# Causal attention on one core: another order of the query blocks, and one block's last norm moved into the recurrence

## The chip, the cores and the metric

The kernel runs on one core of one Trainium2 chip. The metric is the device time of one execution in microseconds (us), taken on the slowest core, of which there is one here. The core has five engines that run their own instruction streams and wait for each other by semaphores: TensorE (PE; its weight loads are listed apart as PEld), VectorE (DVE), ScalarE (ACT), GpSimd (POOL) and SyncE (SP), which here issues most of the DMAs.

## The reference, cut to what matters

The input x has 2 sequences (batches) of 2048 rows of 256 numbers. Six layers add to it in turn:

```
x = x + 0.5 * moe(layernorm(x))
x = x + attention0(layernorm(x))         # full attention, 16 heads
x = x + 0.5 * moe(layernorm(x))
x = x + 0.5 * recurrence(layernorm(x))
x = x + attention1(layernorm(x))         # the changed one
x = x + 0.5 * recurrence(layernorm(x))
```

The changed layer is causal attention with 16 heads of 16 numbers, rotated queries and keys, and a learned vector per clipped distance (-32 to 32) in both the scores and the sum:

```
q, k = rotate(x @ w_q.T) / 4, rotate(x @ w_k.T);  v = x @ w_v.T
rel = rel_emb[clip(key - query, -32, 32) + 32]
scores = q . k + q . rel, masked where key > query
a = softmax(scores)
out = (a @ v + sum over keys of a * rel) @ w_o.T
```

The layer after it, the recurrence, goes over the two sequences as its two steps, row by row of the 2048:

```
c = sigmoid(x@wf.T + c@uf.T + bf) * c + sigmoid(x@wi.T + c@ui.T + bi) * tanh(x@wc.T + c@uc.T + bc)
h = tanh(x @ wo.T + c_last @ uo.T + bo)
```

## The kernel before

**Layout.** x stays on the chip for the whole program as 8 blocks of 512 rows (4 chunks of 128 rows): blocks 0 to 3 are batch 0, blocks 4 to 7 batch 1 (SB = 4 blocks a batch). A layer norm of a block has three calls (L95 to L127): `stats` (mean and variance on DVE, the root on POOL in `root`, `ve` and `rstd`), `normal` (four operations, x to normalised rows `b`) and `turn` (eight transposes on PE and two ACT copies). n4 is the norm ahead of the causal attention, n5 the one ahead of the last recurrence.

**Groups.** `attention1` (from L1008) cuts its work into 32 groups (b, qc, g): batch b, query block qc of 512 queries (the "first" block is qc = 0, the "fourth" qc = 3), and one of G = 4 sets of four heads. The list `groups` fixes their order. Before, each batch has the second block's four groups, then the third block and the first block in turns for pairs of groups (2, 2, 0, 0, 2, 2, 0, 0), then the fourth block's four.

**Units.** Each group is done twice over the keys. The first pass, "largest", makes scores on PE (L1149) and their row maxima on DVE (L1158, and L1179 to L1192 near the diagonal, where the distance term is added from a `band` buffer, of which there are NBAND = 3). The negated maxima `mneg` are transposed and added to the queries by `subtract` (L645). The second pass, "exponential", makes the scores again with keys on the partitions (L1243, L1250, L1260, L1266), takes their exponential on ACT (L1274), and one unit later multiplies by the values in `weighted` (L1283). ACT copies that product to a buffer `part` (L654; five buffers) and POOL adds it to the group's sum one unit later (L552). Each pass of a group takes 4*qc + 3 units: 3 for the first block, 15 for the fourth. A unit may hold a piece of "largest" of one group, a piece of "exponential" of an earlier one, or both; PE's instructions of both are issued in alternation by the loop over units (L1401 to L1424).

**The planner.** The lists Ms and Me (first and last unit of a group's "largest"), Es and Ee (of its "exponential") and By come from fixed rules (L1317 to L1332): "exponential" starts at least three units after the group's "largest" has ended and after the previous group's; "largest" starts when a band buffer is free, and every second group from the sixth on not before the "exponential" of five groups earlier has ended plus nine units:

```
start = max(start, free + 9 - size)
if n > 5 and n % 2 == 0:
    start = max(start, Ee[n - 5] + 9)
...
start = Me[-1] + 3
if n:
    start = max(start, Ee[-1] + 1)
```

**Small jobs.** All else is put into units by distance from those numbers (L1350 to L1398): projections `queries`, `keys` (rotated on POOL, two at a time) and `vals`; the norms of blocks (`ln_stats`, `ln_transpose`); `tables` (cosine and sine of a block, by DMA); `by_position` (distance scores of a group, stored to DRAM and loaded back in skewed form by `band_load`); and after the maxima `band_store`, `positions_load`, `positions_exp`, `positions_T` (four transposes, L1306) and `positions` (one product, L1311), which handle the distance term of the sum. `divide` (L661, transposes at L668) comes at `end = max(Es + 13, Ee + 4)`. When a block's fourth group is divided, `outputs_T` (L682) follows at end + 2 and `outputs`, in two halves (L691), at end + 4 and end + 6; these add the layer's result to x. Jobs that fall behind the last "exponential" unit are simply done one after the other there, a stretch called the drain below. DMA issues that SP makes are `sends` at units of the same plan. At the end the list `tail` (L1551, put into the plan at L1398) adds the norms of blocks 0 and 4 for the last recurrence, at Me of the last group plus 6 to 14 units.

**The last recurrence** (L865 to L1005) has its order written out by hand. Per block cb and step it has a `gate` for each half m (three products, ACT's functions, DVE's state update, L921). Its `normal` and `turn` make a block's norm only where it is not there yet (L891 to L899). The beginning reads:

```
normal(0, 0); first_bias(); turn(0, 0); normal(1, 0)
gate(0, 0, 0); turn(1, 0); gate(0, 0, 1); normal(0, 1)
gate(1, 0, 0); turn(0, 1); gate(1, 0, 1)
```

Here normal(0, 0) is block 0 and normal(0, 1) block 4, the first block of batch 1. `first_bias` (L881) holds the recurrence's first matmuls. Its weights are loaded on SP, issued behind the attention's own DMAs (L1461, L1559).

## Time and profile before

| what | value |
| --- | --- |
| median of 5 runs | 4149.44 us (4145.87 to 4153.36) |
| profiled execution | 4146.6 us, span 4144.8 us |
| mean granted TensorE clock | 0.983 |
| causal attention, from the timeline | 2686.6 to 3961.4 us of the span |
| last recurrence, from the timeline | 3961.4 us to the end |

The profile is one execution. Times in it are us from the start of the span. The page gives each engine's busy time as a share of the span, then the span in 40 slices with the busy tenths of each engine and the granted TensorE clock, then the chain of work that ended last. A group "out<-in" names an instruction by the program's buffers, and Lnnn is the line of the kernel. The view of windows gives the same for any stretch; the timeline gives single instructions or runs of them, with the idle time ahead of them and what ended it.

### The profile page before, as it was taken

What the parts mean: (1) busy time and instruction counts of PE and PEld (TensorE: products, weight loads), DVE (VectorE), ACT (ScalarE), POOL (GpSimd) and SP (SyncE); (2) the same over time, 40 slices, a digit from 0 to 9 for tenths busy, and PEclk for the clock granted to TensorE, in tenths of its full rate; (3) what the DMA queues carried; (4) which work ended last, traced back from release to release, by engine and by line L of the source; (5) the groups of instructions that cost most, each with busy time, mean ns of one, the idle gap of its engine ahead of it and who ended that gap; (6) DMA issues with size and microseconds to landing.
All of it is one profiled execution on the core that took longest, in us unless ns stands there. A gap on an engine that the chain in (4) does not pass through costs nothing.

```text
span 4144.8 us, 78045 instructions
## 1 busy us (share of the span) xinstructions
PE 4003.9 (97%) x29024; PEld 1966.7 (47%) x29024; DVE 2700.2 (65%) x6131; ACT 2555.0 (62%) x5067; POOL 1621.8 (39%) x1421
## 2 busy tenths in 40 slices
PE   7899999999999999999996999999999999999999
PEld 4455433333333433333343554655555455555445
DVE  5234888888877788888742234477767756767634
ACT  2233588888888788888851332256666776676842
POOL 4234233335433333333344123044554564544410
PEclk9899999999999999999998999999999999999999
DMA  7232000100000000000022331054543343542201
GB/s 246 91 117 76 24 2 1 47 1 1 2 1 1 1 1 1 1 1 1 10 92 90 98 108 44 11 113 77 113 95 70 77 83 77 113 95 60 69 1 41
DMA packets 355514, 223.28 MB, mean 54 GB/s; under 512 B 146624, under 2 KB 338496, under 8 KB 355136
## 3 DMA queue, kind: packets, MB, share of 16 engines
q1 hardware_dynamic: 276800, 176.33, 16.7%
q0 software_dynamic: 12288, 33.57, 2.5%
q10 hardware_dynamic: 66048, 8.39, 1.4%
q8 instruction: 231, 3.78, 0.4%
q14 instruction: 147, 1.20, 0.1%
HBM read 113.12 MB, written 105.12 MB: 53 GB/s over the span
## 4 chain that ended last, share of the span: by engine, by line
PE 90%; DVE 4%; another core or an unknown queue 3%; ACT 2%; issue 2%; POOL 0%; DMA 0%; ACTq 0%; DVEq 0%; POOLq 0%
PE s L780 14%; PE s L792 12%; PE s L766 10%; PE s L148 7%; PE s L1149 7%; PE s L1283 7%; PE s L394 6%; PE s L1250 6%; PE s L414 3%; PE s L157 3%; PE s L1260 1%; PE s L691 1%; PE s L1243 1%; PE s L1266 1%
## 5 line engine op out<-in xcount | busy, mean ns | idle before, releaser
L552 POOL TENSOR_TENSOR part<-part 128x512 f32<-128x512 f32 (+2 forms) x768 | 950.1, 1238 | 1395.6 <-ACT part L654 1391.7
L770 DVE TENSOR_REDUCE mx<-s 128x1 f32<-128x512 f32 x2048 | 1271.3, 684 | 301.6 <-PE s L766 290.8
L785 ACT ACTIVATE pT<-s 128x512 f32<-128x512 f32 x2048 | 1063.5, 617 | 197.8 <-PE s L766 194.6
L766 PE MATMUL s<-kT,q 32*128 32x512 f32 x4096 | 1029.4, 617 | 1.7 <-issue 0.8
L780 PE MATMUL s<-q,kT 32*128 32x512 f32 x4096 | 1017.5, 615 | 1.3 <-DVE q L649 1.3
L1274 ACT ACTIVATE pT<-s 128x512 f32<-128x512 f32 (+1 forms) x1152 | 580.6, 584 | 207.7 <-PE s L1250 103.0
L780 PEld LDWEIGHTS s<-q,kT 32*128 32x128 f32 x4096 | 416.0, 183 | 460.9 <-DVE mx L770 376.5
L654 ACT COPY part<-s 128x512 f32<-128x512 f32 (+2 forms) x832 | 500.3, 602 | 164.9 <-PE s L792 58.3
L1158 DVE TENSOR_REDUCE mx<-s 128x1 f32<-128x512 f32 (+1 forms) x768 | 472.7, 679 | 155.4 <-PE s L1149 149.7
L792 PE MATMUL s<-pT,v 128*32 128x512 f32 x4096 | 549.2, 604 | 0.7 <-ACT pT L785 0.2
L766 PEld LDWEIGHTS s<-kT,q 32*128 32x128 f32 x4096 | 410.4, 183 | 140.6 <-ACT pT L785 78.3
L1149 PE MATMUL s<-kT,q 32*128 32x160 f32 (+6 forms) x2240 | 341.3, 429 | 0.0
L394 PE MATMUL s<-we,xT 128*128 x592 | 292.3, 618 | 18.7 <-issue 12.3
L1283 PE MATMUL s<-pT,v 128*32 128x512 f32 (+3 forms) x2560 | 297.3, 539 | 5.0 <-ACT pT L1274 4.8
L401 DVE TENSOR_TENSOR h<-sg,s 128x256 f32<-128x256 f32 x148 | 62.4, 421 | 358.0 <-ACT sg L399 305.9
L1149 PE MATMUL s<-b,q 32*128 32x512 f32 (+7 forms) x1280 | 261.0, 515 | 1.8 <-DVE mx L1158 1.8
L447 POOL DMA_INDIRECT yg<-results,at x128 | 126.1, 985 | 329.0 <-DMA results<-y 243.0
L792 PEld LDWEIGHTS s<-pT,v 128*32 128x32 f32 x4096 | 84.4, 108 | 351.0 <-ACT pT L785 327.6
L1250 PE MATMUL s<-q,kT 32*128 32x512 f32 (+3 forms) x1152 | 242.1, 508 | 0.0
L552 POOL TENSOR_TENSOR band<-band,mneg 128x640 f32<-128x640 f32 x128 | 160.2, 1262 | 154.5 <-DVE mneg L1192 85.0
L1179 DVE CUSTOM_DVE_ANT_0 band<-s,band 128x160 f32<-128x160 f32 (+1 forms) x512 | 153.7, 314 | 96.0 <-PE s L1149 60.8
L1250 PE MATMUL s<-q,b 32*128 32x512 f32 (+3 forms) x896 | 212.0, 568 | 0.0
(227 smaller groups left out, 5181.2 us busy)
## 6 DMA issues: line engine op xcount, KB each, us to landing
band<-skew SPq DMA_DIRECT2D x32, 1280.0 KB
pd<-band SPq DMA_DIRECT2D x32, 1280.0 KB
xs<-places SPq DMA_DIRECT2D x148, 128.0 KB
results<-y SPq DMA_DIRECT2D x148, 128.0 KB
places<-zero SPq DMA_DIRECT2D x2, 4736.0 KB
we<-in_we SPq DMA_DIRECT2D x12, 768.0 KB
skew<-s ACTq DMA_DIRECT2D x32, 256.0 KB
s<-pd SPq DMA_DIRECT2D x32, 256.0 KB
```

The lines of the kernel that those rows point to most:

```text
L394: nc.tensor.matmul(pu, lhsT=xT[n][:, ts(kc, P)], rhs=w[:, kc, ds(val[n], 2 * D)], start=kc == 0, stop=kc == 1,)
L552: fn(*args)
L654: nc.scalar.copy(part[:, q0:], pv[:, q0:])
L766: nc.tensor.matmul(ps, lhsT=q[t][rows(j), ts(qb, P)], rhs=kT[b, g][rows(j), ts(kc, TB)], start=True, stop=True,)
L770: nc.vector.tensor_reduce(mx[t][:, qb * J + j, kc : kc + 1], ps, AX.X, ALU.max)
L780: nc.tensor.matmul(st, lhsT=kT[b, g][rows(j), ts(kb, P)], rhs=q[t][rows(j), :], start=True, stop=True,)
L785: nc.scalar.activation(z.pTs[t, kb, j], st, AF.Exp)
L792: nc.tensor.matmul(pv[rows(j), :], lhsT=v[b, g // 2][:, kb, ds(h * VW, 32)], rhs=z.pTs.pop((t, kb, j)), start=True, stop=True,)
L1149: nc.tensor.matmul(ps[:, ds(cols, n)], lhsT=q[t][rows(j), ts(qb, P)], rhs=kT[b, c, g][rows(j), ds(k0, n)], start=True, stop=True,)
L1250: nc.tensor.matmul(ps[:, q0:], lhsT=k, rhs=q[t][rows(j), q0:], start=True, stop=True, skip_group_check=True,)
L1274: nc.scalar.activation(z.pTs[t, kbs, j][:, q0:], ps[:, q0:], AF.Exp)
L1283: nc.tensor.matmul(pv[rows(j), q0:], lhsT=v[b, kb // CPB, g // 2][:, kb % CPB, ds(h * VW, 32)], rhs=pT[:, ds(c0, TB - q0)], start=kb == kb ...
```

## The change

The first block is no longer alternated with the third block but with the fourth, so that a batch goes second (four groups), third (four groups), then fourth and first in turns for pairs of groups. With this, the last groups of the program are two of the first block of batch 1, and that block's x is complete only at the end of the attention; its norm for the last recurrence leaves the list `tail`, and is made by the recurrence's own `normal(0, 1)` and `turn(0, 1)`. The norm of block 0 stays in `tail`, at Me of the last group plus 2, 4 and 6 units. The tables of the fourth block wait for the projections of the third block where they waited for those of the first.

```
-                groups += [(b, 1, g) for g in range(G)]
+                groups += [(b, qc, g) for qc in (1, 2) for g in range(G)]
                 for g in range(0, G, 2):
-                    groups += [(b, qc, g + i) for qc in (2, 0) for i in range(2)]
-                groups += [(b, 3, g) for g in range(G)]
+                    groups += [(b, qc, g + i) for qc in (3, 0) for i in range(2)]
...
-                    done_ = {2: 1, 3: 0}.get(qc)
+                    done_ = {2: 1, 3: 2}.get(qc)
...
-        tail = []
-        for i, b in enumerate((0, SB)):
-            tail += [(3 + 2 * i, n5.stats, b), (4 + 2 * i, n5.normal, b, nc.vector),
-                     (5 + 2 * i, n5.turn, b)]
+        tail = [(1, n5.stats, 0), (2, n5.normal, 0, nc.vector), (3, n5.turn, 0)]
```

Everything else that moves does so through the planner's rules, which are unchanged.

## The prediction

> **What bounds the kernel now.** I read the page's busy shares first, then its slices, then the chain that ended last: TensorE (PE) is busy 97% of the span and carries 90% of the chain, so a microsecond counts only where PE has less to do or is left waiting.

> ```profile
> PE 4003.9 (97%) x29024; PEld 1966.7 (47%) x29024; DVE 2700.2 (65%) x6131; ACT 2555.0 (62%) x5067; POOL 1621.8 (39%) x1421
> ...
> PE   7899999999999999999996999999999999999999
> ...
> PEclk9899999999999999999998999999999999999999
> ...
> PE 90%; DVE 4%; another core or an unknown queue 3%; ACT 2%; issue 2%; POOL 0%; DMA 0%; ACTq 0%; DVEq 0%; POOLq 0%
> ```

> By the timeline the causal attention runs from 2686.6 to 3961.4, the last recurrence from there to the end. Next, the windows (start:end, length, then busy time and count of PE, PEld, DVE, ACT, POOL; granted clock; DMA share; GB/s), one for 100 us of the attention and three for single units of the plan: "largest" alone, "largest" paired with "exponential", "exponential" alone.

> ```profile
> 3600.00:3700.00 100.00, 99.31 (x956) 57.40 (x949) 70.42 (x238) 69.73 (x138) 51.83 (x44) 1.00 0.56 115
> 2857.68:2859.34 1.66, 1.66 (x14) 0.73 (x13) 1.62 (x8) 0.43 (x3) 0.70 (x2) 1.00 0.00 0
> 3804.30:3807.23 2.93, 2.93 (x26) 1.00 (x25) 2.42 (x5) 1.96 (x5) 1.43 (x2) 1.00 1.16 265
> 3945.69:3948.29 2.60, 2.60 (x20) 0.74 (x16) 0.00 (x0) 2.60 (x7) 0.45 (x2) 1.00 0.00 0
> ```

> PE is full in the paired unit (2.93) with DVE and ACT to spare. Alone, "largest" takes 1.66, all but 0.04 of it DVE's maxima, and "exponential" 2.60, all of it ACT's. So a pair costs 2.93 where the two alone cost 4.26: each further pair saves up to 1.3 us, because a lone unit runs at the pace of DVE or ACT.

> **Part 1, the order of groups.** No matmul of the scores is added or removed; only their places change. I worked the planner's rules (starts, ends, band buffers) through for both orders. Before: 257 units hold both pieces, 31 only "exponential", 31 only "largest". After: 261, 27, 27. So four more pairs. Price: with 2.60 for the lone "exponential" 1.33 each; the fastest one in that stretch starts at 3943.62 and the next at 3945.69, 2.07, which gives 0.80. Four times: −5.3 to −3.2. I take the middle, **−4.2**. Units near the diagonal (band work on DVE) also meet other partners; I fitted the lengths of before's units by kind of piece and by small jobs (residual 0.29 a unit), and these shifts came to +4.5 and −4.1, so I put them at **0 (±2)**.

> **Part 2, the end of the attention.** Before, the last group has 15 units and most of its small jobs fall among them; after, the last two groups are first-block groups of 3 units, and what is due at fixed distances falls behind the last "exponential" unit. Now the view of the stretch behind it and its timeline (start, length, engine, line, operation, wait before):

> ```profile
> 3906.72:3950.75 44.03, 44.03 (x371) 16.73 (x367) 13.57 (x33) 42.75 (x90) 24.34 (x23) 1.00 0.35 88
> 3950.75:3961.37 10.62, 7.83 (x38) 4.86 (x37) 1.38 (x3) 3.65 (x7) 3.38 (x3) 1.00 0.01 2
> ```
> ```profile
> 3955.44 0.66 PE L668 MATMUL s<-ident,part 128*128 128x128 f32 x4 [2.18 <-POOL part L552]
> ...
> 3957.40 0.60 PE L691 MATMUL s<-a_o,b 128*128 128x256 f32 x2
> 3958.24 3.29 PE L691 MATMUL s<-a_o,b 128*128 128x256 f32 x14 [0.24 <-ACT b L685]
> ```

> Before, this drain is 10.62 us, 2.18 of it PE's wait for POOL's last add, and 5.93 from the divide (3955.44) to the recurrence's first matmul (3961.37). After, PE has in turn, by the plan's units: the last "weighted" 1.9; outputs of the fourth block, two halves (0.60 + 3.29 for 16 matmuls, so 3.9); with them the last two groups' transposes of the positions (0.5 each, start to start of four transposes) and positions matmuls (1.1 each); two divides, the first behind a wait of about 1.6 for its ACT copy (0.6) and POOL add (1.2), then 0.5 of its own; and the last chain as before, 2.2 of wait + 5.9. Sum 1.9 + 3.9 + 1.0 + 2.2 + 1.6 + 0.5 + 2.2 + 5.9 = 19.2, that is +8.6. But of this 3.9 + 1.0 + 2.2 + 0.5 = 7.6 no longer stands among the units, where PE had no gap either: −7.6. Net **+1.0**: only the new wait, and the small rest. If the other deferred matmuls slide into the two waits it is −1.8; if each chain waits by itself, up to +4. The loads of the last recurrence's weights on SP stand behind the last band's sends and so start later, but in before they land within 13 us of issue (3919 to 3932), and the longer drain covers that.

> **Part 3, the norm of the first block of batch 1.** Before, statistics, normal and turn of that block stand in the attention; after, its x is ready only at the very end, and the recurrence makes them at its own `normal(0, 1)` and `turn(0, 1)`. The timeline around the same steps of another block in that stage:

> ```profile
> 3978.57 0.75 DVE L921 SCALAR_TENSOR_TENSOR state<-gf,in_c,gi 128x512 f32<-128x512 f32 x1
> 3991.91 0.23 POOL L104 TENSOR_SCALAR ve<-mv 128x4 f32<-128x4 f32 x1 [23.90 <-DVE mv L100]
> ...
> 3993.30 1.38 DVE L117 TENSOR_SCALAR b<-x,mv,rstd 128x256 f32<-128x256 f32 x4 [1.48 <-POOL rstd L106]
> ...
> 3998.85 1.64 PE L127 MATMUL s<-ident,b 128*128 128x128 f32 x8 [0.29 <-DVE b L117]
> ```

> DVE is free for it at 3979.3 (3978.57 + 0.75). The norm takes 2.2 (statistics) + 0.23 + 1.25 (POOL and its wait) + 1.38 = 5.1, so the input of the turn is ready at 3984.4. PE comes to the turn at 3982.1; it would wait 2.3 and then transpose 1.0, less what it gains by later jobs already queued: the next gate starts some **+3.1** later. In the attention PE loses the same eight transposes, **−1.0** (twice 0.5). Bounds: 0 (the wait lies where gates wait for DVE anyway) to +5.1 (nothing hides it). Behind the waiting turn stand only the gate's matmuls; DVE holds no other work that is due. The three POOL instructions that leave the attention are worth nothing to PE.

> **Part 4, tables' buffer and batch change.** The rule `{2: 1, 3: 2}` only delays the cosine loads of block 3 until block 2's rotations are issued. At the change of batch, keys, queries and two norms of the next batch meet on POOL. In before they hide behind two or three units with no stall on PE; I cost it at **0**, and the first rival is what it costs if that cover is gone.

> **Part 5, the granted clock.** Three windows of the attention and one behind it fall to 0.5 to 0.6; two of them (3118 and 3742) follow six "largest" units in a row, where PE is short of work:

> ```profile
> 3110.00:3117.00 7.00, 6.29 (x37) 3.41 (x29) 6.76 (x25) 0.00 (x0) 2.53 (x3) 1.00 0.00 0
> 3117.00:3121.00 4.00, 4.00 (x18) 3.50 (x18) 4.00 (x8) 0.00 (x0) 0.00 (x0) 0.60 1.03 227
> 3964.00:3968.00 4.00, 4.00 (x7) 1.68 (x8) 2.29 (x11) 1.86 (x2) 1.26 (x2) 0.57 0.00 0
> ```

> A window of 3.4 us at half speed loses 1.7. After, the longest run of lone "largest" units is four; the four at units 37 to 40 of before showed no such window. So both may go (−3.4), and the longer drain may bring one more (+1.7): I put −2.0 + 1.7 = **−0.3**, between −3.4 and +5 (the stage's start shows one of 13.7 us, 2704.8 to 2718.5, a loss of 6.8, behind 10 us with PE busy 5.61). [...]

> [...]

> **Sum.** −4.2 + 0 + 1.0 + 3.1 − 1.0 − 0.3 = −1.4 us on the profiled execution of 4146.6 (span 4144.8), which stands 2.8 under the median of 4149.44. So 4145.2 for a profile, and **4148 us** against the median.

> **Rivals.** (a) *Slower by a stall at the change of batch.* After, two norms (0.23 + 1.04 + 4.85 each), two rotation steps and a band add are all due on POOL in one unit, 15.9 us in a unit of 4.4, while the adds of `part` (1.24 each) queue behind them, and there are five `part` buffers.

> ```profile
> 3192.08 4.85 POOL L117 TENSOR_SCALAR b<-x,mv,rstd 128x256 f32<-128x256 f32 x4
> ...
> 3203.18 3.71 POOL L552 TENSOR_TENSOR part<-part 128x512 f32<-128x512 f32 x3
> ```

> Before has 12.6 us there (3190.6 to 3203.2) with no stall on PE, which speaks against; for it, the cover is three units, 10.6 us at the fitted lengths, and the new batch's band chain, copy to first use, has 15.5 us where the shortest of before has 17.5. It decides when the add issued three units earlier ends later than ACT comes to reuse its buffer. Price up to 15.9 − 4.4 = 11.5 us: −1.4 + 11.5 gives 4159.5, with a clock window more 4166. (b) *Faster:* four pairs at the top (−5.3), both half-speed windows gone without a new one (−3.4), deferred matmuls filling the drain's waits (−1.8), the recurrence's turn at +1 net 0: −10.5, so 4139; with two more from the near units and the recurrence covered, 4134. (c) *The change does not do what it says:* pairs save nothing because what a lone unit leaves idle is used by its neighbours; then 4148 + 4.2 = 4152, still within the forecast's case.

> **How the numbers follow.** 0.2% is 8.3 us, about what a measurement here can tell from no change. Forecast with (c) 0.50; (a) 0.30, since three covers must hold there (the units', the buffers', the band chain's); (b) 0.20, since four terms must all come in at their favourable end. (a) and (b) each lie mostly past 8.3 us, so faster 0.20, within 0.50, slower 0.30. To leave out no more than 2 in 10 the range reaches both, 4134 to 4166; the forecast's own is 4142 to 4157.

> **What would show it.** Right: paired stretches still 99 to 100 busy per 100 us; some 4 us less between the stage's start and the last "exponential" unit beside the 8.6 us of moved jobs; a drain of about 19 us; the first wait of PE on `b` of L117 2 to 3 us at the second gate of the recurrence; no 0.6 window after lone "largest" units. Wrong: any wait of PE on ACT or POOL of several us near the first units of batch 1 (a), or a drain that repeats the 2.18 wait more than twice.

## The result, and the profile after

The changed kernel is slower. Its median is 4157.9 us (28 runs) beside 4149.56 us for the kernel before (49 runs): a ratio of 1.0021 with a 95% interval of 1.0016 to 1.0026, or +8.3 us. The forecast was 4148, a gain of 1.4. The time lies inside the stated range of 4134 to 4166, but on the other side of no change, and not for the reason of the first rival.

The page of the changed kernel, the lines that answer to those of before:

```profile
PE 4008.3 (97%) x29024; PEld 1964.3 (47%) x29024; DVE 2699.0 (65%) x6131; ACT 2553.4 (62%) x5067; POOL 1617.5 (39%) x1421
...
PE   7799999999999999999987999999999999999999
...
PEclk9899999999999999999997999999999999999999
...
PE 90%; DVE 4%; another core or an unknown queue 2%; ACT 2%; issue 1%; POOL 0%; DMA 0%; ACTq 0%; DVEq 0%; POOLq 0%
```

The same 29024 matmuls are there, and nothing on this page tells the two kernels apart. The span is 4151.2 against 4144.8, so the two profiled executions differ by 6.4. The windows of four stretches show where: up to the first paired unit, from there to the end of the last "exponential" unit, the drain, and the last recurrence. First before, whose drain of 10.62 the prediction shows, then after (columns as in the prediction).

```profile
2686.60:2732.68 46.08, 39.89 (x278) 21.59 (x277) 37.61 (x106) 14.41 (x26) 19.00 (x19) 0.85 0.27 70
2732.68:3950.75 1218.07, 1211.65 (x11499) 681.11 (x11497) 837.49 (x2514) 839.68 (x1651) 618.14 (x522) 1.00 0.41 86
...
3961.37:4144.80 183.43, 176.37 (x553) 99.46 (x551) 74.66 (x156) 50.25 (x77) 7.60 (x12) 0.98 0.07 23
```
```profile
2686.60:2732.45 45.85, 38.73 (x277) 21.39 (x270) 37.59 (x106) 14.19 (x26) 18.86 (x19) 0.89 0.27 68
2732.45:3947.64 1215.19, 1204.93 (x11450) 668.60 (x11448) 829.54 (x2496) 836.53 (x1646) 614.76 (x518) 1.00 0.42 86
3947.64:3966.57 18.93, 14.68 (x77) 10.78 (x77) 4.73 (x9) 4.98 (x10) 4.25 (x4) 0.91 0.02 7
3966.57:4151.20 184.63, 176.33 (x561) 99.71 (x559) 77.96 (x168) 51.29 (x79) 8.86 (x14) 0.99 0.07 23
```

The drain and the recurrence are longer by 8.3 and 1.2; a half-clock window, a loss of 1.7, lies in the drain after (at 3960.88) and in the recurrence before (at 3964.32), and without it they are longer by 6.6 and 2.9, for 8.6 and 3.1 forecast. The units should have been shorter by 12.8 (4.2 + 7.6 + 1.0); they are shorter by 2.9. In them TensorE now waits 1215.19 - 1204.93 = 10.26 us, where it waited 6.42. The view of TensorE's waits, from the first paired unit to the recurrence, names the new ones (us in total, times, longest), before and after:

```profile
PE s L1283 <- ACT pT L1274: 4.8, 8, 0.7
PE s L668 <- POOL part L552: 2.2, 1, 2.2
PE s L645 <- DVE mneg L1192: 1.4, 2, 0.7
```
```profile
PE s L1282 <- ACT pT L1273: 4.7, 8, 0.7
PE s L645 <- DVE mneg L1191: 4.6, 4, 1.7
PE s L668 <- POOL part L552: 3.8, 2, 2.1
```

The wait of `subtract` for the negated maxima, VectorE's last work on a group, has grown from 1.4 to 4.6: four times 0.6 to 1.7 us, one for each lone "largest" stretch of four units (37 to 40, 85 to 88, 191 to 194, 239 to 242). Here is the first of these stretches, before and after. It does the same pieces of "largest" in both kernels.

```profile
2852.45:2864.46 12.01, 12.01 (x107) 6.37 (x107) 11.67 (x39) 1.45 (x5) 10.10 (x9) 1.00 0.33 66
```
```profile
2852.23:2867.76 15.53, 14.90 (x107) 6.99 (x107) 13.96 (x44) 1.44 (x5) 7.63 (x7) 0.89 0.53 77
```

Both hold 107 matmuls, but 12.01 us have become 15.53: 0.63 idle, VectorE busy 13.96 where it was 11.67, and a granted clock of 0.89 on average, which is a loss of 0.11 x 15.53 = 1.7. The timelines show what differs. Before:

```profile
2855.24 1.92 PE L157 MATMUL s<-b,a_q 128*32 128x512 f32 x16
2857.09 0.66 PE L1306 MATMUL s<-ident,s 128*128 128x128 f32 x4
2857.68 1.14 PE L1149 MATMUL s<-b,q 32*128 32x512 f32 x8
2858.75 0.66 PE L645 MATMUL s<-ident,mneg 128*128 128x128 f32 x4
2859.34 2.44 PE L1149 MATMUL s<-b,q 32*128 32x512 f32 x8
```

After:

```profile
2857.42 0.55 PE L645 MATMUL s<-ident,mneg 128*128 128x128 f32 x3
2858.60 0.33 PE L645 MATMUL s<-ident,mneg 128*128 128x128 f32 x1 [0.63 <-DVE mneg L1191]
2858.86 2.72 PE L1148 MATMUL s<-b,q 32*128 32x512 f32 x8
2861.51 3.43 PE L157 MATMUL s<-b,a_k 128*32 128x512 f32 x16
2864.87 2.20 PE L614 MATMUL s<-a_v,b 128*128 128x128 f32 x16
```

Before, a projection of queries (16 matmuls, 1.92) stands ahead of `subtract`, and while TensorE does it VectorE gets through the maxima of the two near units; `subtract` then finds its input ready. After, the 16 projection matmuls of this stretch are keys, due two units later, behind `subtract`. TensorE arrives early, waits 0.63, and the clock then drops (to 0.50 for 3.41 us, from 2861.79): the 16 matmuls that took 1.92 take 3.43.

**Theory G** is therefore: the loss lies in the stretches of lone "largest" units, where VectorE sets the pace and a small wait of TensorE is often followed by a window of half clock. **Rivals**: theory P (a pair saves nothing), theory E (the loss is at the end: drain and moved norm), and rival D (within G, only VectorE's amount of work counts, not the place of TensorE's jobs).

### The profile page after: what moved, and what is told of

Read it like the earlier page. It is cut to its first block, busy times and chain, and to the rows that moved or that the text cites. A ratio compares the mean times of both kernels' runs of the same rounds, so it can differ in the third digit from the quotient of the medians.

```text
span 4151.2 us, 78015 instructions
## 1 busy us (share of the span) xinstructions
PE 4008.3 (97%) x29024; PEld 1964.3 (47%) x29024; DVE 2699.0 (65%) x6131; ACT 2553.4 (62%) x5067; POOL 1617.5 (39%) x1421
## 4 chain that ended last, share of the span: by engine, by line
PE 90%; DVE 4%; another core or an unknown queue 2%; ACT 2%; issue 1%; POOL 0%; DMA 0%; ACTq 0%; DVEq 0%; POOLq 0%
PE s L780 14%; PE s L792 12%; PE s L766 10%; PE s L148 7%; PE s L1148 7%; PE s L1282 6%; PE s L394 6%; PE s L1249 5%; PE s L414 3%; PE s L157 3%; PE s L691 1%; PE s L1259 1%; PE s L1242 1%; PE s L1265 1%
## 5 line engine op out<-in xcount | busy, mean ns | idle before, releaser
L552 POOL TENSOR_TENSOR part<-part 128x512 f32<-128x512 f32 (+2 forms) x768 | 947.8, 1235 | 1413.4 <-ACT part L654 1410.8
L552 POOL TENSOR_TENSOR band<-band,mneg 128x640 f32<-128x640 f32 x128 | 160.0, 1260 | 130.7 <-DVE mneg L1191 98.3
```

The lines of the kernel that those rows point to most:

```text
L552: fn(*args)
```

## The experiments

The kernels were run in three groups, each beside runs of the kernel before on the same chip. In the second and third group the layers ahead of the attention took some 130 us less, in the kernel before too, so ratios are compared (why they took less, no run here shows); the attention's unedited parts have the same lengths there to 0.1 us. "Stage" below is the time from the first paired unit to the recurrence's first matmul: 1228.69 in the profile of before, 1234.12 in that of after.

**The changed kernel again** (no edit).

> The changed kernel once more, unedited, for a second profile. Theory G (stretches of lone largest units): in both profiles the granted clock falls to about 0.5 for 3.4 us right behind the lone largest units of the third and fourth block's first groups (near 2862, 3055, 3682; perhaps near 3490 too), since VectorE sets the pace there and TensorE waits. If the windows of half clock lie elsewhere in this execution, or are absent, G is wrong on their cause.

One profile, no interval. The stage took 1233.96 and the recurrence 184.66, and the unit stretches repeat to 0.1 us. The half-clock windows are behind the same three stretches (37 to 40, 85 to 88, 239 to 242), none at 191 to 194: as G has it.

**New order for batch 0 alone.**

```
+                if b == 0:
+                    groups += [(b, qc, g) for qc in (1, 2) for g in range(G)]
+                    for g in range(0, G, 2):
+                        groups += [(b, qc, g + i) for qc in (3, 0) for i in range(2)]
+                    continue
                 groups += [(b, 1, g) for g in range(G)]
...
-                    done_ = {2: 1, 3: 0}.get(qc)
+                    done_ = {2: 1, 3: 0 if b else 2}.get(qc)
```

> New order for batch 0 alone; batch 1, the end of the attention and both norms as before. The plan has 257 paired units, as before. Theory G: the lone largest stretches of batch 0 cost, in idle time of TensorE and half clock, 0.63 + 1.71 + 1.66 + 1.68 = 5.7 us where before has 0.71 + 1.67 = 2.4, so +3.3 us: about 4153. Theory P (pairs save nothing, nothing else is wrong) and theory E (the loss is at the end: drain and moved norm): no change, 4149.5. The first rival of the prediction (stall at the change of batch) would show a wait of TensorE of several us near the first units of batch 1, +5 to +11.

Ratio 1.0013 (1.0004 to 1.0022), +5.5 us. With the number of pairs, the end and both norms as before, a loss is there that can be most of the change's (the interval runs from 1.7 to 9.1 us): P and E alone cannot be the cause. No wait of several us appears at the change of batch; TensorE's waits from 3150 to 3380 are 1.7 us in all, on ACT.

**New order for batch 1 alone, with the new end.** The same edit with b == 1 and the changed list `tail`.

> New order for batch 1 alone, with its end and with block 4's norm in the recurrence; batch 0 as before. The plan has 261 paired units. Theory G with pairs worth 1.05 each as predicted: -4.2 + 1.0 (drain) + 1.9 (norm) + 1.0 (one stretch of 3.3 for one of 2.4) = -0.3, so 4149. G and P: +3.9, so 4153. Theory E: all of the change's +8, so 4158.

Ratio 0.9997 (0.9988 to 1.0006), -0.5 us: the first of the three numbers. The half of the change that holds the longer drain, the moved norm and the four more pairs costs nothing in sum. Theory E falls. The two halves add up to +5.0 beside the +8.3 of the whole, which the intervals allow; the profiles are added up below.

From the first paired unit to the drain, with batch 0 and with batch 1 alone in the new order:

```profile
2733.03:3955.08 1222.05, 1213.37 (x11498) 677.42 (x11496) 837.05 (x2514) 838.61 (x1651) 617.00 (x522) 1.00 0.40 86
```
```profile
2729.06:3935.22 1206.16, 1199.04 (x11450) 669.94 (x11449) 827.23 (x2493) 836.79 (x1646) 615.44 (x518) 1.00 0.41 86
```

**Only the norm moved.**

```
-        tail = []
-        for i, b in enumerate((0, SB)):
...
+        tail = [(3, n5.stats, 0), (4, n5.normal, 0, nc.vector), (5, n5.turn, 0)]
```

> Order as before; only block 4's norm moves from the attention into the recurrence. All theories but E: +2.9 in the recurrence (wait of the turn and its transposes) less 1.0 of transposes in the attention, +1.9: about 4151.5. Theory E: up to +5 (the whole chain of the norm). Nothing at all if the gates have slack there.

Ratio 1.0001 (0.9992 to 1.0010), +0.3: the interval, some 3.7 us to either side, holds the expected 1.9 and 0 alike. The profile is sharper: the turn waits, as in the changed kernel, 1.26, and the recurrence takes 186.37 where before has 183.43, each with one half-clock window in it.

```profile
3958.76 1.04 PE L127 MATMUL s<-ident,b 128*128 128x128 f32 x8
3971.35 1.65 PE L127 MATMUL s<-ident,b 128*128 128x128 f32 x8 [1.26 <-DVE b L117]
```

The first of these lines is block 1's turn, whose input is ready; the second is block 4's.

**One projection two units later, in the order of before.**

```
-                at(early[n], queries, n)
+                at(early[n] + 2 * (n == 8), queries, n)
```

> Order as before; only one projection of queries (16 matmuls) moves from the second to the fourth unit of the lone largest stretch 37 to 40, where the changed order has its keys. Theory G (the clock falls when the near units of such a stretch hold no other work for TensorE): the stretch, 12.01 us in before with no idle time, gets an idle gap near 0.6 and a half-clock window (1.7 lost): about 14.3. Rival D (the changed order's 15.53 comes from the two norm statistics that VectorE has more of there): it stays at 12.0 to 12.3.

The stretch 37 to 40 of this kernel:

```profile
2722.96:2736.31 13.35, 12.72 (x107) 6.68 (x107) 12.98 (x41) 1.45 (x5) 6.58 (x7) 1.00 0.41 70
```
```profile
2729.34 0.33 PE L645 MATMUL s<-ident,mneg 128*128 128x128 f32 x1 [0.63 <-DVE mneg L1192]
```

One profile, no interval. One job moved by two units takes 12.01 to 13.35 and makes the very wait of 0.63. VectorE is busy longer in the longer stretch (12.98 beside 11.67), but it reaches the negated maxima that `subtract` waits for at the same time, 6.15 us after the start of the stretch, before and here:

```profile
2858.60 0.17 DVE L1192 TENSOR_REDUCE mneg<-mx 128x4 f32<-128x16 f32 x1
```
```profile
2729.11 0.17 DVE L1192 TENSOR_REDUCE mneg<-mx 128x4 f32<-128x16 f32 x1
```

Up to there only the place of TensorE's work differs. Rival D falls as the whole cause. The window that G expected did not come in this execution, so the 14.3 were missed: a wait of 0.63 does not bring it each time.

**Norm statistics three units later, in the changed order.**

```
-                            at(f - 34 + 2 * c, z.ln_stats, b, qc, c)
+                            at(f - 34 + 2 * c + 3 * (qc == 3), z.ln_stats, b, qc, c)
```

> The changed kernel with the fourth block's norm statistics three units later, out of the stretches 37 to 40 and 191 to 194. Rival D (VectorE's amount of work sets those stretches): each gets 1.2 shorter (two statistics of 0.6), the window at 37 to 40 may stay: 15.5 to 14.3, 13.9 to 12.7; about -2.4 of 4150. If the stretch stays at 15.5, the order of PE's own work sets it and not VectorE's amount.

Ratio 1.0021 (1.0012 to 1.0031), no different from the changed kernel. The stretch 37 to 40 is 13.36, this time without a window. Without a window and with the statistics it is 13.89 in the profile of the kernel with the early norm (below). So VectorE's statistics are worth 0.53 and not 1.2: of the two only one stands ahead of maxima of the stretch, where the eight score matmuls behind `subtract` take 2.72 with it and 2.19 without. D holds for that part. The stretch 191 to 194, for which 12.7 was expected, is 15.00, with a window; without its 1.7 that is 13.3, the same as the first. Now the first stretch is whole: 12.01 + 1.34 (place of the projection) + 0.5 (statistics) + 1.7 (window) = 15.55, and 15.53 was measured.

**Filler matmuls where TensorE waits.** The kernel does extra work here that nothing reads.

```
+            warm = {4: 6, 8: 14, 20: 6, 24: 14}
+            def keep_warm(k):
+                pb = bank()
+                for i in range(k):
+                    nc.tensor.transpose(pb[:, ts(i % CPB, P)], ident, ident)
...
+                if n in warm:
+                    jobs.at(Me[n] + 1, keep_warm, warm[n])
                 jobs.at(Me[n] + 1, z.subtract, n)
```

> The changed kernel with extra transposes of the identity, read by nobody, ahead of the subtract jobs in the four lone largest stretches: 6 (about 0.7 us) at units 39 and 193, 14 (about 1.7 us) at 87 and 241, as much as TensorE waits there. Theory G (a half-clock window follows TensorE's idle time): idle time there goes to 0, the stretches keep their length (VectorE sets it), and the three windows go: -3 x 1.7 = -5 us against the changed kernel, ratio to before 1.0008. Rival (the window has another cause, such as the little work of the near units): windows stay, ratio 1.002 or, with the extra work in the way, more.

The stretches 37 to 40 and 85 to 88 with the fillers, and 85 to 88 of the changed kernel:

```profile
2722.06:2736.55 14.49, 14.49 (x113) 7.63 (x113) 13.88 (x44) 1.45 (x5) 7.18 (x7) 1.00 0.47 76
...
2913.25:2926.20 12.95, 12.82 (x111) 7.77 (x111) 11.57 (x38) 3.40 (x7) 8.17 (x8) 1.00 0.37 81
```
```profile
3044.47:3058.48 14.01, 12.35 (x98) 6.28 (x97) 11.65 (x38) 3.40 (x7) 8.74 (x8) 0.88 0.43 89
```

Idle time is gone but for 0.13, and with it all windows of the four stretches in this profile: as G has it. The fillers themselves cost 0.6 a stretch beyond the idle time they fill (14.49 against 13.89). The whole did not get faster: ratio 1.0021 (1.0011 to 1.0030). The expected gain of 5 did not come. In this profile three windows fewer (-5.1) are mostly paid back by the fillers (four times 0.6) and by the half clock behind the units, which came twice (3826 and 3837) and not once (+1.7): about 1 is left, which the interval cannot tell from nothing.

**The new order's stretches filled with real work.**

```
                         due = f - 14 if qc == 0 else f - 10 - 2 * (f < 12)
+                        if qc == 2 and g:
+                            due -= 3
...
                         due = Es[index[b, max(qc, 1), 2 * half]] - 2 + 2 * (qc == 0)
+                        if qc > 1 and not half:
+                            due -= 2
```

> The changed kernel with the keys of units 40 and 194 three units earlier and the first values of the third and fourth block two units earlier, so that the lone largest stretches hold matmuls from their start. Theory G: no half-clock window behind 2850, 3045, 3675 and idle time near 0 there; VectorE's busy time then bounds the stretches: 15.5 to 14.0, twice 14.0 to 11.7, 13.9 to 13.5, together -6.5 us: ratio to before about 1.0005. Rival (the windows come from something else, such as the start of the next band work): windows stay, no gain, ratio 1.002.

Ratio 1.0024 (1.0013 to 1.0035): not the hoped 1.0005. The wait of 0.63 stayed and that of 1.66 became 1.76, because keys and values bring VectorE work of their own (a shuffle, an addition), which stands ahead of the maxima there, and because VectorE stands idle for it and for the next scores, which now come behind the projections on TensorE. In the first stretch these are three waits, 1.7 us in all:

```profile
2725.95 0.01 DVE L1044 LOAD_MASK_SELECT s<-kT  x1 [0.80 <-ACT kT L1042]
...
2727.22 0.69 DVE L622 TENSOR_TENSOR v<-s,a_rel_row 128x512 f32<-128x512 f32 x1 [0.52 <-PE s L614]
2728.28 0.33 DVE L1178 CUSTOM_DVE_ANT_0 band<-s,band 128x160 f32<-128x160 f32 x1 [0.36 <-PE s L1148]
```

In these stretches the wait was away where TensorE's work stood behind the scores of the near units and ahead of `subtract` and brought VectorE little (the projection in before, 12.01 us without a wait); here, where keys and values stood ahead of those scores, 0.63 and 1.76 were left.

**The values alone, two units earlier, in the order of before.** The second of the two edits above.

> The kernel before with the first values of the third and fourth block two units earlier. Theory G: the stretches 99 to 104 and 253 to 258 lose their 0.71 of idle time each and their half-clock windows (1.55 each where they occurred): -2 to -4.5 us. Rival: no change.

Ratio 0.9993 (0.9984 to 1.0002), -3.1 us, just not clear of no change. The stretch 99 to 104 lost its idle time and its window, 20.89 to 17.94:

```profile
3101.27:3122.16 20.89, 20.18 (x151) 14.11 (x151) 19.16 (x66) 4.15 (x10) 9.41 (x8) 0.92 0.27 55
```
```profile
2971.54:2989.48 17.94, 17.94 (x151) 12.31 (x151) 16.78 (x63) 4.11 (x10) 9.41 (x8) 1.00 0.09 26
```

Without a window the stretch of before takes 19.2 (20.89 less 1.7), so 1.3 of this is gained without half clock. Over all units, half clock taken out, only 0.7 remains (1214.0 beside 1214.7): the rest of the gain, if it is one, is windows that did not come.

**Four pairs fewer.**

```
+                start += 4 * (n == 29)
                 Es.append(start)
```

> The kernel before with the exponential pass of the 30th group four units late: 253 paired units instead of 257, four lone largest units at 274 to 277 and four more lone exponential units at the end, nothing else changed. As predicted (a pair saves 0.8 to 1.33): +3.2 to +5.3, and 1.7 more if the four lone units bring a half-clock window. Theory P (pairs save nothing): 0.

Ratio 1.0019 (1.0010 to 1.0028), +6.6. From unit 259 to the recurrence's first matmul, the same 1857 matmuls, first this kernel and then before:

```profile
3617.09:3838.46 221.37, 218.50 (x1857) 107.15 (x1856) 131.97 (x332) 163.22 (x323) 96.27 (x81) 0.99 0.27 56
```
```profile
3747.58:3961.37 213.79, 210.92 (x1857) 103.82 (x1855) 132.38 (x330) 163.49 (x323) 96.35 (x81) 1.00 0.25 57
```

+7.58, of which 1.7 is a half-clock window (3833 to 3837) that before has a little later, in the recurrence. That leaves 5.9, or 1.47 a pair. Theory P falls, and the price in the prediction (0.80 to 1.33) was if anything too small. The four lone units at 274 to 277 are far ones, TensorE does not wait there, and no window followed.

**The norm early in the recurrence**, in the changed kernel.

```
             normal(1, 0)
+            normal(0, 1)
             gate(0, 0, 0)
...
             gate(0, 0, 1)
-            normal(0, 1)
```

> The changed kernel with the recurrence making block 4's norm right after block 1's, ahead of the first gate, instead of after the second. As the prediction's step 3 has it, the recurrence loses 2.9 because the turn waits for the norm (1.26 in the trace) and does its eight transposes (1.0, and 0.6 of pipeline behind the wait): -1.3 to -1.9. No change if another wait takes its place (VectorE late with the first gate's state).

Ratio 1.0021 (1.0012 to 1.0030), no different from the changed kernel within the interval. In the profile the wait ahead of the turn is gone and the recurrence takes 182.64 against 184.63, with the half clock ahead of it in both: -2.0, just more than was expected.

```profile
3860.79 1.04 PE L127 MATMUL s<-ident,b 128*128 128x128 f32 x8
```

**The parts that gain, together.** New order for batch 1, the early norm, and the first values of batch 0's fourth block two units earlier:

```
+                        if b == 0 and qc == 3 and not half:
+                            due -= 2
```

> New order for batch 1 alone, the early norm in the recurrence, and the fourth block's first values of batch 0 two units earlier (which took idle time and window out of stretch 99 to 104). From the parts: batch1 -0.5 measured, -1.6 for the norm, -1.4 to -3.0 for the stretch: -3.5 to -5 against before, ratio 0.999. If the parts do not add, 1.000.

Ratio 0.9988 (0.9979 to 0.9997), -4.6 us: faster than the kernel before by 0.1%, as forecast from the parts.

## Why the prediction was wrong

Here the two profiled executions are compared with the time lost to half clock taken out (a stretch's length times what its granted clock lacks of 1), since the windows come and go between executions. Only the stretch up to the first paired unit is given whole.

| step | forecast | measured |
| --- | --- | --- |
| units, four more pairs, regrouping, moved jobs | -4.2 + 0 - 7.6 - 1.0 = -12.8 | 1210.1 - 1214.7 = -4.6 |
| drain | +8.6 | 17.2 - 10.6 = +6.6 |
| recurrence | +3.1 | 184.6 - 181.7 = +2.9 |
| half clock, lone "largest" stretches | -2.0 | 5.1 - 3.4 = +1.7 |
| half clock, drain and recurrence | +1.7 | 0 (1.7 in both) |
| up to the first paired unit | 0 | -0.2 |
| sum | -1.4 | +6.4 |

**The step that failed is part 1**, its term for the units that meet other partners, "0 (±2)", together with the lone price. That pairing is worth 0.8 to 1.33 was right, if anything too small (1.47 measured). The units were forecast to lose 12.8 and lost 4.6, so 8.2 is missing (more, if a pair saved the 1.47). Two experiments measure the term by halves. With half clock taken out (3.4 and 2.1), new order in batch 0 alone, which has no pair more and no job moved to the end, takes 1218.6 for the units beside 1214.7: +4.0 for a term put at 0. New order in batch 1 alone takes 1204.1, or -10.6 where -12.8 was forecast: +2.2, as far as the prices of pairs and moved jobs hold. The other 2.0 come only with both.

I priced all lone units alike, by one far unit, and counted them: 31 and 31 before, 27 and 27 after. What a lone unit costs depends on its place. A lone "largest" stretch is VectorE's, as the row 1.66 with 1.62 of VectorE already said; so what counts in it is VectorE's backlog from the near units, what VectorE gets besides, and whether TensorE has other work ahead of `subtract`. The change moves exactly these. Without half clock, stretch 37 to 40 rose by 1.8, and stretch 191 to 194 stands at 13.89 where the kernel with new order in batch 0 alone, whose projection is still in the second unit, has 12.01. For these two, 3.7 together, the cause is shown above. The waits at 85 to 88 and 239 to 242 are 1.66 each, where the stretches they replace had 0.71; that is at most 1.9 more, and the stretches hold other pieces, so it is not as closely shown. The remaining 2.6 or so of the 8.2 was not traced to its place: a fit of the units' lengths by kind and small jobs puts about this much into the lone "exponential" stretches, but that is an estimate, and no run tried it.

**Part 5 failed in its sign.** I expected the windows to go because the longest lone run shrinks from six units to four, and because the four at 37 to 40 of before had none. The length of the run was the wrong sign to read: in those four TensorE did not wait (busy 12.01 of 12.01 us), thanks to a projection in the second unit. After the change it does wait (0.63). The prediction also misread a row there: the 10 us with TensorE busy 5.61 are 2700 to 2710, half of them inside the half-clock window that begins at 2704.8; in the 10 us ahead of it TensorE was busy 7.44.

**What held.** The drain, worked out item by item as 19.2, took 18.93, with the two waits for POOL as foreseen. The sum came out so close in part by luck: a half-clock window of 1.7 is in it, and the last "weighted" took 0.9 where I had put 1.9.

```profile
3955.68 0.66 PE L668 MATMUL s<-ident,part 128*128 128x128 f32 x4 [1.63 <-POOL part L552]
3956.17 1.02 PE L1310 MATMUL s<-s,relv 128*128 128x512 f32 x2
3959.33 0.66 PE L668 MATMUL s<-ident,part 128*128 128x128 f32 x4 [2.13 <-POOL part L552]
...
3966.57 0.95 PE L881 MATMUL s<-in_c,uf 128*128 128x1 f32 x8
```

The moved norm cost 2.9 for 3.1, here too with errors that cancel: the wait at the turn was 1.26 and not 2.3, but the turn behind it took 1.65 and not 1.0. The first rival, a stall on POOL at the change of batch, has no trace: the cover held. The second rival had pairs at their top price, and they were worth that, but the other places of the units took more. The third was wrong, as four fewer pairs showed.

From +6.4 in the two profiles to +8.3 in the medians: the profiled execution of before had a window in both its stretches of six, but in all executions of those stretches that were profiled unedited it came in 4 of 10. The new stretches have it more often (below). With 0.8 windows of 1.7 in before and some 2.6 in after, +4.7 without windows becomes about 7.8. This is an estimate from few executions, and it leaves out the half clock at the start of the attention, which varies too (a loss of 6.8 and of 5.1 in the two profiles).

## What to carry to other kernels

When two streams of work are interleaved by a plan, do not count the units in which one stands alone: look in each such stretch for the engine that paces it, what small jobs fall into it and in which order they stand against the first instruction that waits for the pacing engine. Work that fills such a wait must not stand ahead of what feeds the pacing engine (here it made 1.66 of wait into 1.76). A job moved by two units was worth as much here as a pair. And a short wait on a nearly full TensorE should be priced with the half clock that may follow it, 1.7 us here, as much as the longest of these waits.

## What the runs showed of the hardware

Windows of half clock of 3.41 us followed waits of TensorE of 0.63 to 1.76 us, far shorter than the window, and not each time. Over the profiles of all kernels, by the idle time in a lone "largest" stretch: with 1.66 to 1.76 us a window came in 11 of 13 cases, with 0.71 in 4 of 10, with 0.63 in 5 of 12; with no idle time, or 0.13, in none of 15 stretches of four or six units.

```profile
2861.79:2865.20 3.41, 3.41 (x17) 0.76 (x10) 3.40 (x6) 0.21 (x1) 0.00 (x0) 0.50 1.22 166
```
```profile
3960.91:3964.32 3.41, 3.41 (x28) 3.25 (x28) 0.87 (x4) 0.00 (x0) 0.00 (x0) 1.00 0.00 0
```

The lengths of unit stretches repeat to a few hundredths of a us between executions and chips when no window falls into them (the one ahead of units 85 to 88 took 62.50 to 62.52 in six profiles of the new order in batch 0, from at least three chips): one profile was enough to tell 0.5 us in a stretch of 13, where 11 timed runs leave 3.5 us on either side of the median's ratio.
